# A transformer layer and a graph-attention layer in fp32: four projections by seven products of quarters, attention in 8 units instead of 12

## The chip, the cores and the metric

The kernel runs on one core of a Trainium2 chip. The metric is the device time of one launch in microseconds (us). The engines are named as in the profile: PE (TensorE), DVE (VectorE), ACT (ScalarE), POOL (GpSimd).

## The reference

There are 32 independent batches of 512 rows and 512 features, all in fp32, with a sparse adjacency matrix of 512 x 512 that is shared by all of them.

```python
# x (32, 512, 512), adj (512, 512); 8 heads of 64
h = relu(layernorm(x))
q, k, v = h @ Wq + bq, h @ Wk + bk, h @ Wv + bv          # per head below
attn = softmax(q @ k.T / 8 + (1 - adj) * -1e9)
x = x + (attn @ v) @ Wo + bo
h = relu(layernorm(x))                                    # layer 1
g = h @ W
e = leaky_relu(g @ a1 + (g @ a2).T, 0.2) * adj
h_prime = softmax(e) @ g
x = x + elu(h_prime + beta * g)
```

Per batch there are four projections (q, k, v and Wo), attention in four pairs of heads, and for layer 1 a gather (`pg`) and a last product (`py`).

## The kernel before

Batches are pipelined. While batch b does its attention, batch b+1 is projected, batch b-1 goes through Wo and its second normalisation, and batch b-2 ends. TensorE's order is written by hand. The order of the other engines is set at build time by a scheduler, from its own estimate of when each operand is ready. VectorE, ScalarE and GpSimd then take their instructions in that order: in this kernel's trace 3323, 1670 (activations and copies) and 1517 of them stand in the order of the built program, none out of it.

The names in the profiles are those of tiles: `pn` are the transposes of x ahead of the projections (the "turn" in the code), `ps` the scores, `e` the masked scores and then their exponentials, `es` the sums of these, `po` the values, `pd` the denominators, `pbs` a row of logits spread over all rows.

```python
psum = ... bufs=2                      # three tags: mm (1 bank), s (2 banks), o (1 bank), two buffers each

def product(nc, out, lhsT, rhs, start=True, stop=True):      # two halves of 64 columns side by side
    for s in range(0, out.shape[0], HD):
        nc.tensor.matmul(out[s : s + HD], lhsT[:, s : s + HD], rhs, start=start, stop=stop)

def proj_k(b, hT, f, kT):                                    # one of 4 blocks; q, v and Wo alike
    p = psum.tile([P, N], F32, name=f"pk_{b}_{f}", tag="mm")
    for c in range(C):
        product(nc, p, wk[:, c, ts(f, P)], hT[c], start=c == 0, stop=c == C - 1)
    k = wtile([P, N], f"kT_{b}_{f}", "kT", 6)
    nc.scalar.activation(k, p, AF.Identity, bias=bk_c[:, f : f + 1])

def scores(b, j, k, st):
    p = psum.tile([P, 2, N], F32, name=f"ps_{b}_{j}_{k}", tag="s")
    ...                                                       # two matmuls of 512 columns
    e = wtile([P, 2, N], f"e_{b}_{j}_{k}", "e", 6)
    nc.vector.tensor_tensor(e, p, nmT[:, k, :]..., op=ALU.add)   # adds the mask, frees the bank
    nc.scalar.activation(e, e, AF.Exp)
    ...                                                       # GpSimd sums e over k into es

# attention: 12 units a batch, three per pair of heads; dense groups are spread evenly between them
units.append(lambda j=j: (scores(b, j, 0, s), scores(b, j, 1, s)))
units.append(lambda j=j: attend(b, j - 1, s))
units.append(lambda j=j: (scores(b, j, 2, s), scores(b, j, 3, s)))

def norm0(b, xs):                                             # layer norm ahead of the projections
    for t in range(T):
        ...                                                   # DVE statistics, POOL power of -0.5
        nc.vector.tensor_scalar(xs[t], xs[t], mv[:, 0:1], rstd, op0=ALU.subtract, op1=ALU.mult)
```

After Wo, each of the four row blocks has its normalisation: statistics on DVE, a power on POOL, a relu on ACT, and two reductions `scr` on DVE. The logits of layer 1 follow (`at`, eight DVE instructions and four exponentials).

Of the kernel before, what the change touches and what calls it, by code (L numbers as in the profile page):

```python
# [17 lines left out]
P = 128  # L18
# [15 lines left out]
def product(nc, out, lhsT, rhs, start=True, stop=True):  # L34


    for s in range(0, out.shape[0], HD):
        nc.tensor.matmul(out[s : s + HD], lhsT[:, s : s + HD], rhs, start=start, stop=stop)  # L38
# [8 lines left out]
def kernel(  # L47
# [34 lines left out]
    wq, wk, wv, wo, w1 = (ctile([P, C, D], n) for n in ("wq", "wk", "wv", "wo", "w1"))  # L82

    def load_w(w, ap):
        nc.scalar.dma_start(w, ap.rearrange("(c p) f -> p c f", p=P))
# [27 lines left out]
    def row_bcast(psum, work, col, name):  # L113

        dg = work.tile([P, T, P], F32, name="dg" + name, tag="dg", bufs=1)
        nc.vector.tensor_tensor(
            dg, ident.unsqueeze(1).to_broadcast([P, T, P]),
            col.unsqueeze(2).to_broadcast([P, T, P]), op=ALU.mult,
        )
        p = psum.tile([P, N], F32, name="pb" + name, tag="mm")  # L120
        product(nc, p, ones, dg.rearrange("p t n -> p (t n)"), start=True, stop=True)
        return p
# [6 lines left out]
    psum = fast.enter_context(tc.tile_pool(name="psum", bufs=2, space=bass.MemoryType.PSUM))  # L129
# [22 lines left out]
    def masks():  # L152
        for k in range(T):
            p = psum.tile([P, N], F32, name=f"pa_{k}", tag="mm")
# [15 lines left out]
    def row_constants():  # L170

        nc.gpsimd.dma_start(c_row, bcast_rows(bo, D))
        p = psum.tile([P, D], F32, name="pc", tag="mm")
        for c in range(C):
            r = wtile([P, P], f"bvr_{c}", "y", 3)
            nc.vector.tensor_copy(r, bv_c[:, c : c + 1].to_broadcast([P, P]))
            product(nc, p, r, wo[:, c, :], start=c == 0, stop=c == C - 1)
        nc.vector.tensor_add(c_row, c_row, p)
        wa = wtile([P, 2, C], "wa", "wa", 1)
        for g in range(2):  # L180
            ar = wtile([P, D], f"a_{g}", "x1", 6)
# [36 lines left out]
    def turn(b, xs, hT, c):  # L218
        p = psum.tile([P, N], F32, name=f"pn_{b}_{c}", tag="mm")
        for t in range(T):  # L220
            nc.tensor.transpose(p[:, ts(t, P)], xs[t][:, ts(c, P)], ident)
        h = wtile([P, N], f"hT_{b}_{c}", "T", 12)
        nc.scalar.activation(h, p, AF.Relu)
        hT.append(h)

    def proj_q(b, hT, f, qT):
        p = psum.tile([P, N], F32, name=f"pq_{b}_{f}", tag="mm")
        for c in range(C):
            product(nc, p, wq[:, c, ts(f, P)], hT[c], start=c == 0, stop=c == C - 1)
        q = wtile([P, N], f"qT_{b}_{f}", "qT", 6)  # L230
        nc.vector.scalar_tensor_tensor(  # L231
            q, p, bq_c[:, f : f + 1], edge8, op0=ALU.add, op1=ALU.mult
        )
        qT.append(q)

    def proj_k(b, hT, f, kT):
        p = psum.tile([P, N], F32, name=f"pk_{b}_{f}", tag="mm")
        for c in range(C):
            product(nc, p, wk[:, c, ts(f, P)], hT[c], start=c == 0, stop=c == C - 1)
        k = wtile([P, N], f"kT_{b}_{f}", "kT", 6)  # L240
        nc.scalar.activation(k, p, AF.Identity, bias=bk_c[:, f : f + 1])  # L241
        kT.append(k)

    def proj_v(b, hT, t, v):
        p = psum.tile([P, D], F32, name=f"pv_{b}_{t}", tag="mm")
        for c in range(C):
            product(nc, p, hT[c][:, ts(t, P)], wv[:, c, :], start=c == 0, stop=c == C - 1)
        s = wtile([P, D], f"v_{b}_{t}", "v", 8)
        nc.scalar.mul(s, p, VS)
        v.append(s)  # L250

    def scores(b, j, k, st):

        p = psum.tile([P, 2, N], F32, name=f"ps_{b}_{j}_{k}", tag="s")
# [5 lines left out]
        e = wtile([P, 2, N], f"e_{b}_{j}_{k}", "e", 6)  # L260
# [5 lines left out]
        if k == 1:  # L266
            st["es"][j] = wtile([P, 2, N], f"es_{b}_{j}", "es", 2)
# [5 lines left out]
    def attend(b, j, st):  # L273

        po = psum.tile([P, N], F32, name=f"po_{b}_{j}", tag="o")
        e, v = st["e"][j], st["v"]
        for k in range(T):
            for s in range(2):
                nc.tensor.matmul(  # L279
                    po[s * HD : (s + 1) * HD, :],  # L280
                    v[k][:, (2 * j + s) * HD : (2 * j + s + 1) * HD],
                    e[k][:, s, :], start=k == 0, stop=k == T - 1,
                )
        pd = psum.tile([P, N], F32, name=f"pd_{b}_{j}", tag="o")
# [4 lines left out]
        o = wtile([P, N], f"oT_{b}_{j}", "T", 12)  # L289
        nc.scalar.copy(o, po)  # L290
        rd = wtile([P, N], f"rd_{b}_{j}", "rd", 2)
        nc.vector.reciprocal(rd, pd)  # L292
        junk = wtile([P, N], f"rj_{b}_{j}", "rj", 1)
        nc.scalar.activation(junk, rd, AF.Copy, accum_out=rsum[:, b, j : j + 1])
        nc.gpsimd.tensor_tensor(o, o, rd, op=ALU.mult)  # L295
        st["oT"].append(o)

    def residual(b, st):

        st["x1"] = []  # L300
        for t in range(T):
            r = wtile([P, D], f"x1_{b}_{t}", "x1", 6)
            nc.sync.dma_start(r, x[b, ts(t, P), :])
            nc.gpsimd.tensor_tensor(r, r, c_row, op=ALU.add)  # L304
            st["x1"].append(r)

    def out_proj(b, t, st):
        p = psum.tile([P, D], F32, name=f"pw_{b}_{t}", tag="mm")
        for c in range(C):
            product(  # L310
                nc, p, st["oT"][c][:, ts(t, P)], wo[:, c, :], start=c == 0, stop=c == C - 1
            )
        x1 = st["x1"][t]
        nc.vector.scalar_tensor_tensor(x1, p, 1.0 / VS, x1, op0=ALU.mult, op1=ALU.add)  # L314

        if t == 0:
            st["mv"] = wtile([P, T, 2], f"mv1_{b}", "mv1", 2)
        mv = st["mv"][:, t, :]
        rstd = wtile([P, 1], f"rs1_{b}_{t}", "rs1", 4)
        stats(x1, t, f"b{b}", mv, rstd)  # L320
        nb = wtile([P, 1], f"nb_{b}_{t}", "nb", 4)
        nc.vector.scalar_tensor_tensor(nb, mv[:, 0:1], -1.0, rstd, op0=ALU.mult, op1=ALU.mult)
        hn = wtile([P, D], f"hn_{b}_{t}", "hn", 4)
        nc.scalar.activation(hn, x1, AF.Relu, bias=nb, scale=rstd)  # L324
        st["hn"].append(hn)
        if t == 0:
            st["s12"] = wtile([P, 2, T], f"s12_{b}", "s12", 2)
        for g, r in ((0, wa1_r), (1, wa2_r)):
            scr = wtile([P, D], f"scr_{b}_{t}_{g}", "y", 3)
            nc.vector.tensor_tensor_reduce(  # L330
                scr, hn, r, 1.0, 0.0, op0=ALU.mult, op1=ALU.add,
                accum_out=st["s12"][:, g, t : t + 1],
            )
# [19 lines left out]
    def diagonal(b, st):  # L353

        pd = psum.tile([P, T, HD], F32, name=f"pe_{b}", tag="mm")
# [15 lines left out]
    def gather(b, c, st):  # L371
        p = psum.tile([P, N], F32, name=f"pg_{b}_{c}", tag="mm")
# [4 lines left out]
        g = wtile([P, N], f"gT_{b}_{c}", "T", 12)  # L377
# [3 lines left out]
    def final(b, t, st):  # L381
        p = psum.tile([P, D], F32, name=f"py_{b}_{t}", tag="mm")
# [10 lines left out]
        nc.gpsimd.tensor_tensor(y, y, st["x1"][t], op=ALU.add)  # L393
# [5 lines left out]
    def new_state(b):  # L399
        states[b] = {  # L400
            "x": load(b), "hT": [], "qT": [], "kT": [], "v": [], "e": [[] for _ in range(NP)], "es": {},
            "oT": [], "hn": [], "at": [], "gT": [],
        }

    def front_groups(b):
        s = states[b]
        for f in range(C):
            yield lambda f=f: proj_q(b, s["hT"], f, s["qT"])
            yield lambda f=f: proj_k(b, s["hT"], f, s["kT"])
        for t in range(T):  # L410
            yield lambda t=t: proj_v(b, s["hT"], t, s["v"])

    def dense(b):


        def of(n, make, count=4):
            if n is None:
                return [None] * count
            return [lambda i=i: make(n, i) for i in range(count)]

        nxt = b + 1 if b + 1 < B else None
        prev = b - 1 if 0 <= b - 1 < B else None
        old = b - 2 if b >= 2 else None
        s, so = states.get(prev), states.get(old)
        G = of(old, lambda n, c: gather(n, c, so))
        Y = of(old, lambda n, t: final(n, t, so))
        W = of(prev, lambda n, t: out_proj(n, t, s))
        F = list(front_groups(nxt)) if nxt is not None else [None] * 12
        V = F[8:]
        L = [(lambda: (new_state(b + 2), norm0(b + 2, states[b + 2]["x"]))) if b + 2 < B else None]  # L430
        lg = of(prev, lambda n, i: logits(n, s), 1)
        D = of(prev, lambda n, i: diagonal(n, s), 1)
        if b == B:
            order = G + Y[:2] + W + Y[2:3] + lg + Y[3:] + D + [judge]
        else:
            order = (
                G + [Y[0], F[0], Y[1], F[1], W[0], Y[2], W[1], F[2], W[2], Y[3], W[3], F[3], F[4]]
                + L + [F[5]] + lg + [F[6], F[7]] + V[:2] + D + V[2:]
            )
        return [g for g in order if g is not None]  # L440

    def attention(b):

# [268 lines left out]
```

## Time and profile before

| | before |
|---|---|
| time, median | 4039.0 us (4037.9 to 4042.4, 4 runs) |
| steady period, one batch | 123.29 us (28 periods) |
| everything else (start and end) | 586 us |
| TensorE busy | 96% |
| half clock in the steady part | 13.7 us in all |

The "period" is the distance between the transposes `pn` of successive batches in TensorE's timeline. Here it is taken over the 28 batches from the fourth on, because the steps before and after those lack one stage of the pipeline or another. These are rows of the page's costliest groups. Behind the bar stand the busy time, the mean of one in ns, and the idle time just before them with what ended most of it.

```profile
L261 DVE TENSOR_TENSOR e<-ps,nmT 128x1024 f32<-128x1024 f32 x512 | 606.7, 1216 | 431.0 <-PE ps L257 419.6
L257 PE MATMUL ps<-qT,kT 64*128 64x512 f32 x2048 | 522.4, 625 | 6.1 <-DVE e L261 4.1
```

VectorE waits 420 us for scores, while TensorE waits 4.1 us in the whole run for a bank that VectorE has to free.

### The profile page before, as it was taken

The page shows a single profiled execution, that of the slowest core. Times are in us where ns is not written, and L with a number is a line of the kernel's source. Part 1 is how long each engine was busy: PE and PEld are TensorE (multiplying, and loading weights), DVE is VectorE, ACT ScalarE, POOL GpSimd, SP SyncE. Part 2 cuts the span into 40 slices and gives each one's busy share as a digit, 9 for nine tenths or more (in the row PEclk, how much of TensorE's full clock was granted, in tenths as well). Part 3 has the DMA queues.
Part 4 walks back from the last instruction along what each step waited for, and adds up shares of the span by engine and source line. Part 5 has one row for each costly group of instructions (what it writes and reads, how often), then busy time and mean ns, then how long its engine had stood idle before and what let it go on. Part 6 is the DMA issues. An engine that isn't in the chain of part 4 may idle for free. (4 is left out here: it accounts for less than half of the span.)

```text
span 4038.4 us, 45341 instructions
## 1 busy us (share of the span) xinstructions
PE 3886.6 (96%) x18094; PEld 1303.7 (32%) x18094; DVE 2428.3 (60%) x3323; ACT 1258.4 (31%) x1799; POOL 1843.7 (46%) x1519
## 2 busy tenths in 40 slices
PE   6999999999999999999999999999999999999977
PEld 2333333333333333333333333333333333333322
DVE  4556665566655566655666555666556665556653
ACT  1333323333223333333332233333333322333331
POOL 2444544445444445444444444454444444444451
PEclk9999999999999999999999999999999999999989
DMA  3000010001010000110000100001000000000000
GB/s 117 11 17 26 22 32 27 27 21 32 22 32 27 27 22 22 32 30 23 22 32 21 32 27 26 23 21 32 32 21 22 32 21 32 27 27 11 21 21 27
DMA packets 59100, 110.75 MB, mean 27 GB/s; under 512 B 6465, under 2 KB 6465, under 8 KB 58881
## 3 DMA queue, kind: packets, MB, share of 16 engines
q1 hardware_dynamic: 55872, 101.74, 8.1%
q10 hardware_dynamic: 2640, 5.24, 0.4%
q8 instruction: 144, 2.36, 0.3%
q0 software_dynamic: 368, 0.79, 0.1%
q14 instruction: 76, 0.61, 0.1%
HBM read 74.19 MB, written 33.55 MB: 27 GB/s over the span
## 5 line engine op out<-in xcount | busy, mean ns | idle before, releaser
L271 POOL TENSOR_TENSOR es<-es,e 128x512 f32<-128x512 f32 x512 | 715.0, 1427 | 447.5 <-ACT e L264 447.5
L261 DVE TENSOR_TENSOR e<-ps,nmT 128x1024 f32<-128x1024 f32 x512 | 606.7, 1216 | 431.0 <-PE ps L257 419.6
L264 ACT ACTIVATE e<-e 128x1024 f32<-128x1024 f32 x512 | 540.6, 1056 | 906.9 <-DVE e L261 869.2
L292 DVE RECIPROCAL rd<-pd 128x512 f32<-128x512 f32 x128 | 429.4, 3355 | 430.5 <-PE pd L286 430.5
L257 PE MATMUL ps<-qT,kT 64*128 64x512 f32 x2048 | 522.4, 625 | 6.1 <-DVE e L261 4.1
L38 PE MATMUL pq<-hT,wq 128*64 128x512 f32 x2048 | 464.6, 596 | 13.9 <-ACT kT L241 12.9
L38 PE MATMUL py<-w,gT 128*64 128x512 f32 x2048 | 467.6, 599 | 0.5 <-DVE qT L231 0.5
L271 POOL TENSOR_TENSOR es<-e,e 128x512 f32<-128x512 f32 x256 | 344.7, 1368 | 267.6 <-ACT e L264 267.6
L38 PE MATMUL pw<-wo,oT 128*64 128x512 f32 x2048 | 462.8, 594 | 3.3 <-DVE x L314 3.3
L38 PE MATMUL pk<-hT,wk 128*64 128x512 f32 x2048 | 463.0, 594 | 1.1 <-DVE at L341 1.1
L279 PE MATMUL po<-e,v 128*64 128x512 f32 x2048 | 462.6, 594 | 0.0
L38 PE MATMUL pg<-at,hn 128*64 128x512 f32 x2048 | 453.7, 596 | 0.0
L38 PE MATMUL pv<-wv,hT 128*64 128x512 f32 x2048 | 450.8, 593 | 0.0
L295 POOL TENSOR_TENSOR oT<-oT,rd 128x512 f32<-128x512 f32 x128 | 172.0, 1344 | 598.3 <-DVE rd L292 530.8
L304 POOL TENSOR_TENSOR x<-x,c_row 128x512 f32<-128x512 f32 x128 | 166.1, 1299 | 393.4 <-DMA x<-in_x_dram 349.5
L330 DVE CUSTOM_DVE_ANT_0 scr<-hn,wa_r 128x512 f32<-128x512 f32 x256 | 277.7, 1121 | 64.8 <-ACT hn L324 64.6
L393 POOL TENSOR_TENSOR y<-y,x 128x512 f32<-128x512 f32 x128 | 162.4, 1269 | 290.4 <-DVE y L392 290.4
L257 PEld LDWEIGHTS ps<-qT,kT 64*128 64x128 f32 x2048 | 176.5, 188 | 328.0 <-issue 222.1
L391 DVE TENSOR_SCALAR y<-y 128x512 f32<-128x512 f32 x128 | 124.6, 974 | 242.8 <-ACT y L390 242.8
L38 PEld LDWEIGHTS pq<-hT,wq 128*64 128x64 f32 x2048 | 141.3, 137 | 321.0 <-issue 259.6
L38 PEld LDWEIGHTS pw<-wo,oT 128*64 128x64 f32 x2048 | 147.0, 137 | 298.0 <-issue 291.6
L279 PEld LDWEIGHTS po<-e,v 128*64 128x64 f32 x2048 | 147.4, 138 | 292.8 <-issue 292.2
(95 smaller groups left out, 3153.3 us busy)
## 6 DMA issues: line engine op xcount, KB each, us to landing
x<-in_x_dram SPq DMA_DIRECT2D x256, 256.0 KB, 3.0
out_dram<-y SPq DMA_DIRECT2D x128, 256.0 KB, 3.0
wq<-in_L_gnn_Wq_dram ACTq DMA_DIRECT2D x1, 1024.0 KB, 6.9
wk<-in_L_gnn_Wk_dram ACTq DMA_DIRECT2D x1, 1024.0 KB, 14.2
adj<-in_adj_dram SPq DMA_DIRECT2D x4, 256.0 KB, 11.9
wv<-in_L_gnn_Wv_dram ACTq DMA_DIRECT2D x1, 1024.0 KB, 12.2
wo<-in_L_gnn_Wo_dram ACTq DMA_DIRECT2D x1, 1024.0 KB, 14.4
w<-in_L_gnn_W_dram ACTq DMA_DIRECT2D x1, 1024.0 KB, 13.0
```

The source lines that it names most:

```text
L38: nc.tensor.matmul(out[s : s + HD], lhsT[:, s : s + HD], rhs, start=start, stop=stop)
L257: nc.tensor.matmul(p[:, s, :], st["kT"][j][rows, ts(k, P)], st["qT"][j][rows, :], start=True, stop=True)
L261: nc.vector.tensor_tensor(e, p, nmT[:, k, :].unsqueeze(1).to_broadcast([P, 2, N]), op=ALU.add)
L264: nc.scalar.activation(e, e, AF.Exp)
L271: nc.gpsimd.tensor_tensor(es[:, s, :], one[:, s, :], e[:, s, :], op=ALU.add)
L279: nc.tensor.matmul(po[s * HD : (s + 1) * HD, :], v[k][:, (2 * j + s) * HD : (2 * j + s + 1) * HD], e[k][:, s, :], start=k == 0, stop=k == ...
L292: nc.vector.reciprocal(rd, pd)
L295: nc.gpsimd.tensor_tensor(o, o, rd, op=ALU.mult)
L304: nc.gpsimd.tensor_tensor(r, r, c_row, op=ALU.add)
L330: nc.vector.tensor_tensor_reduce(scr, hn, r, 1.0, 0.0, op0=ALU.mult, op1=ALU.add, accum_out=st["s12"][:, g, t : t + 1],)
L391: nc.vector.tensor_scalar(y, y, 1.0, -1.0, op0=ALU.min, op1=ALU.add)
L393: nc.gpsimd.tensor_tensor(y, y, st["x1"][t], op=ALU.add)
```

## The change

Strassen's method (in Winograd's form) makes a product of 2 x 2 blocks with seven block products, not eight, and more additions. Here blocks are 256 x 256. The products are accumulated in PSUM, and partial results are handed on by ScalarE copies between banks ("seeds"). The blocks of the weights are combined once, those of the tokens once per batch on GpSimd. Seven blocks of each weight matrix take more SBUF than the four that make up the matrix, and the ring of exponentials shrinks from 6 to 4. The attention is recut in 8 units, each of two scores and half of the values, so that fewer exponentials live at once (this reason is read from the diff). The diff, cut to its core:

```diff
-    psum = fast.enter_context(tc.tile_pool(name="psum", bufs=2, space=bass.MemoryType.PSUM))
+    psum = fast.enter_context(tc.tile_pool(name="psum", bufs=1, space=bass.MemoryType.PSUM))
...                                                  # tags now: x, y, po, pd (1 bank each), s, qz (2 banks each)
+    def combos(b, name, pairs, tag):
+        b11, b12, b21, b22 = (block(pairs, k) for k in range(4))
+        t2, t3, t4 = (wtile([P, 2, H], f"{name}{i}_{b}", tag, 3) for i in (2, 3, 4))
+        nc.gpsimd.tensor_tensor(t3, b22, b12, op=ALU.subtract)
+        nc.gpsimd.tensor_tensor(b12, b12, b11, op=ALU.subtract)
+        nc.gpsimd.tensor_tensor(t2, b22, b12, op=ALU.subtract)
+        nc.gpsimd.tensor_tensor(t4, t2, b21, op=ALU.subtract)
...
+    def seven(name, w, B, tokens, one, two):
...                                                  # times(): 8 matmuls of 256 columns, 16 records in the profile
+        x_ = tile1("x")
+        times(x_, A11, "b11", True)
+        y_ = tile1("y")
+        nc.scalar.copy(y_, x_)
+        yield
+        qz = psum.tile([P, 2, N], F32, name=f"qz_{name}", tag="qz")
+        z_ = qz[:, 1, :]
+        times(qz[:, 0, :], S1, "t1", True)
+        q_ = wtile([P, N], f"q5_{name}", "q5", 1)
+        nc.scalar.copy(q_, qz[:, 0, :])
+        yield
+        times(y_, S2, "t2", False, onto=True)
+        nc.scalar.copy(z_, y_)
+        yield
+        times(x_, A12, "b21", False, onto=True)
+        one(0, 0, x_)
+        yield
+        times(z_, S3, "t3", False, onto=True)
+        two(1, 1, z_, q_)
+        yield
+        times(y_, S4, "b22", False, onto=True)
+        two(0, 1, y_, q_)
+        yield
+        times(z_, NA22, "t4", False, onto=True)
+        one(1, 0, z_)
...
-        e = wtile([P, 2, N], f"e_{b}_{j}_{k}", "e", 6)
+        e = wtile([P, 2, N], f"e_{b}_{j}_{k}", "e", 4)
...
+    def unit(b, n, tags=("qz", "s")):
+        s = states.get(b)
+        j, second = divmod(n, 2)
+        if s is not None:
+            for k in range(2):
+                scores(b, j, 2 * second + k, s, tags[k])
...
+    def step(b):
...
+        def strassen(pieces, n=1, between=None):
+            for i, _ in enumerate(pieces):
+                if i == 0:
+                    att(n, ("qz", "s"))              # a unit after the first product
+                if i == 4 and between:
+                    between()
...                                                  # v, unit 1, gather and final with units 2 to 4
+        if nxt is not None:
+            turn(b + 1, nxt)
...
+        if prev is not None:
+            strassen(out_proj(b - 1, prev))          # unit 5
...
+        if b + 2 < B:
+            new_state(b + 2)
+            norm0(b + 2, states[b + 2]["x"])
+        if nxt is not None:
+            strassen(proj_k(b + 1, nxt))             # unit 6
+        if prev is not None:
+            logits(b - 1, prev)
+        if nxt is not None:
+            strassen(proj_q(b + 1, nxt))             # unit 7
```

## The prediction

> **What bounds the kernel now.** I read the page's first two parts for the bound, then TensorE's waits, then the timeline for where a batch spends its time.
>
> ```profile
> PE 3886.6 (96%) x18094; PEld 1303.7 (32%) x18094; DVE 2428.3 (60%) x3323; ACT 1258.4 (31%) x1799; POOL 1843.7 (46%) x1519
> PE   6999999999999999999999999999999999999977
> PEclk9999999999999999999999999999999999999989
> L38 PE MATMUL pk<-hT,wk 128*64 128x512 f32 x2048 | 463.0, 594 | 1.1 <-DVE at L341 1.1
> ```
>
> TensorE is busy all the way, at full clock; the loads of weights (PEld) lie under it. A busy PE is not proof, so I ask what it waits for:
>
> ```profile
> PE pbs L38 <- DVE qT L231: 51.5, 28, 3.2
> PE pn L221 <- DVE x L214: 21.6, 1, 21.6
> PE pe L38 <- POOL as L351: 13.0, 2, 8.7
> PE pq L38 <- ACT kT L241: 12.9, 24, 0.5
> ```
>
> Beside the start and the end, TensorE waits only 1.8 us (51.5 / 28) and 0.5 us in a batch. So it is bound by the number of columns that it streams. The transposes pn, once a batch, start at 1985.85, 2108.95 and 2231.87 us in the timeline; over 28 batches (260.3 to 3712.5) the period is 123.3 us. Start and end take the other 586 us.
>
> The pitch, from the PE timeline:
>
> ```profile
> 2001.67 7.04 PE L38 MATMUL pg<-at,hn 128*64 128x512 f32 x32
> 2008.63 1.99 PE L257 MATMUL ps<-qT,kT 64*128 64x512 f32 x8
> 2101.47 0.69 PE L38 MATMUL pe<-ones,as 128*64 128x64 f32 x16
> 2101.99 1.46 PE L38 MATMUL pv<-wv,hT 128*64 128x512 f32 x6
> ```
>
> Each half of 64 columns is two records, and two halves run side by side. 32 records take 6.96 us from start to start, less some 0.1 us for the change of tile form: 429 ns for a side-by-side pair of 512 columns. 16 records of 64 columns take 0.52 us, 58 ns in the steady part. A line through both gives 217 ns for a pair of 256 columns (an estimate: 5 ns fixed, 0.83 ns a column).
>
> [...]So halving the columns loses almost nothing. [...]after a wait of 3.19 us (pbs at 1461.76) the clock was 0.50 for 3.41 us. [...]scr takes 626 to 1779 ns, the long ones beside POOL work.
>
> **The change part by part.**
>
> Removed: a projection was 64 records of 512 columns, 32 pairs x 429 = 13.74 us. Seven products of 16 records of 256 columns are 56 pairs x 217 = 12.17 us. Four projections a batch: 6.3 us saved, 201 us in all. TensorE's own need falls from 119.5 to 113.2 us: 48.7 for projections, 27.5 for gather and final, 33.4 for eight units of attention (scores 1.92, half of the values 1.8, denominators 0.86 every second unit), 3.6 for the small ones. The units' count moves no work; it sets how far apart scores stand.
>
> Added on other engines, per batch: three ScalarE copies of 580 ns a projection, 7.0 us; eight GpSimd combinations of 1.3 to 1.4 us, 11 us, and four half-width multiplications, 3 us; VectorE some 5 us (kT and v partly moved to it, two more adds for x1). Busy would be DVE 81, POOL 72, ACT 44 of some 125 us: none becomes the bound by its sum. The seeds (copy of x into y, of y into z) have a 1.74 us product between them and their use, against about 0.8 us for copy and semaphore: hidden, when the engine's queue is free.
>
> Moved, and this decides: scores had two buffers of two banks beside two banks for projections. Now one of their two buffers, qz, is also where Strassen's products go, and each scores unit in a projection puts its first tile into qz. The next product must wait until VectorE has added the mask to that tile. VectorE takes its instructions in the built order. I read this order for one batch: in front of the mask-add of unit 6 (in the k projection, just after Wo) stand all of the normalisation after Wo, four rows, and nearly all of that before the batch after next. Before, a row of it stood between projections.
>
> The groups that matter there:
>
> ```profile
> L330 DVE CUSTOM_DVE_ANT_0 scr<-hn,wa_r x256: 626/694/1779, 190.6 to 3986.5; 128x512 f32<-128x512 f32 x128
> L195 DVE BATCH_NORM_STATS2 st_b<-x x128: 686/695/698, 186.5 to 3983.0; 128x6 f32<-128x512 f32 x128
> 2060.90 0.68 DVE L195 BATCH_NORM_STATS2 st_a<-x 128x6 f32<-128x512 f32 x1
> 2077.31 2.34 DVE L261 TENSOR_TENSOR e<-ps,nmT 128x1024 f32<-128x1024 f32 x2
> ```
>
> I walk from the end of Wo's sixth product, where y is complete, with start-to-start times (a little under durations). VectorE: semaphore 0.2; two adds 1.3; add from z 0.65; eight statistics x 0.6 = 4.8; eight reductions scr x 0.62 = 5.0, undisturbed; twenty small ones 1.5; two of the four scalings of x 0.95; the mask-add 1.2; waits for GpSimd's power some 0.7: 16.3 us. TensorE meanwhile has the seventh product 1.74, k's first 1.74, scores 1.92, values 1.8, denominators 0.86, and 0.4 for z: 8.4 us. It then stands for **7.9 us in each batch**, before k's second product.
>
> Others found in the same walk: Wo's first product writes the bank x, which the last transposes have just filled, and ScalarE's four relus (0.6 each) end 1.25 us after them: 1.25 us. In the q projection, the mask-add of unit 7 stands behind the eight logits instructions (pbs to the last: 5.1 us, some 7 with GpSimd's sums beside them), and TensorE has only 5.5 us of work: 3.0 us. z of Wo: 0.45 us. [...]the clock will halve in most batches; some 3.4 us of work at half speed cost 1.7 us.
>
> Sum: 113.2 + 7.9 + 1.25 + 3.0 + 0.45 + 1.7 = 127.5 us a batch against 123.3. Over 28 batches +118 us. Start and end: four batches of smaller products, -25 us; masks through one bank, back-to-back units in the first step, and a longer normalisation chain in the last, +15 to +20. Prediction 4150 us.
>
> **The rivals.** First: the saving arrives. If VectorE had the mask-add done in time, only small waits would remain: 113.2 + 5 = 118 us, 3890 us in all. For it: VectorE is busy 60% and 65% after, and before the trace shows scores hardly ever waiting (ps for e 4.1 us in all). Against it: in the timeline of before, the scores that ended by 2072.1 got their mask-add at 2077.31. VectorE was already 5 us behind at this very place, and a second buffer hid it.
>
> Second: GpSimd becomes the pace. 58 us become 72, [...]eight scr at 1.7 instead of 0.65 would be +8 us, the stand near 16 us, the time 4370 us. Against it: by the walk GpSimd has ended the sums of unit 5 before the normalisation begins, and only the short powers are left. In the trace of before a power came late once a batch (3.34 us behind es), so some of it may come.
>
> Third: the stand is real but partly paid back, because VectorE's backlog is worked off and the waits before pbs (1.8 us) are gone. I have counted their absence already. Without the clock's fall it would be 4100 us, which counts as the same.
>
> **Range and chances.** 1 us a batch is 28 us. I give the period plus or minus some 4.5 us, mostly for the stand and the clock: 4010 to 4290. Faster by over 2% needs a period below 120.6, that is the stand almost gone; the durations used are already the undisturbed ones, so 0.12, for a misread order. Within 2% (120.6 to 126.4): 0.33. Slower: 0.55.
>
> **What would show it.** Right: a row of qz of the k projection waiting for e (DVE) about 30 times with 6 to 10 us each; PEclk below 9 in many slices; the seven products' rows near 390 us each for Wq, Wk, Wv, Wo instead of 460; PE's share near 90%; a smaller wait of qz of q for e; x of Wo waiting for ACT hT near 1.2 us. Wrong: pitch of pairs of 256 columns well above 217 ns (then no saving at all); waits of TensorE under 5 us a batch (first rival); scr means above 1.3 us with POOL near full beside them (second rival); ScalarE's copies (y or qz) as the main releaser.

## The result

The changed kernel is correct and took 4155.1 us (median of 4 runs, 4154.6 to 4157.9) against 4039.0 us. The ratio is 1.0287, with a 95% interval of 1.027 to 1.0305: slower. A ratio is the mean time of one kernel's fast runs over the mean of the other's fast runs of the same rounds, so it is not quite the ratio of the medians quoted. The prediction said 4150 us and slower with 0.55.

The busy line and two slices of the page of the changed kernel:

```profile
PE 3737.9 (90%) x24302; PEld 1771.4 (43%) x24302; DVE 2362.5 (57%) x3712; ACT 1402.5 (34%) x2119; POOL 2180.0 (52%) x1922
PE   5998999988999888999889999889998889998977
PEclk7999999999999999999999999999999999999998
```

TensorE's busy time fell by 149 us while the span grew by 118 us. TensorE was given less to do and does it later. No engine is near full, so the time must lie in waits. TensorE's waits in the changed kernel (engine, waiting tile, releaser: total us, times, longest):

```profile
PE qz_k L46 <- DVE e L400: 212.5, 30, 7.5
PE qz_q L46 <- DVE e L400: 47.6, 30, 1.6
PE pn L275 <- ACT hT L283: 25.9, 32, 1.6
...
PE x_w L46 <- ACT hT L286: 21.4, 29, 0.7
PE qz_k L46 <- POOL hT L263: 12.3, 1, 12.3
```

The first row is the one foreseen: k's second product waits until VectorE has added the mask to a tile of scores. Of its 30 times 28 lie in the steady part and take 7.5 us each (210.3 / 28); the 7.1 us that the expectations below name is the mean with two short ones of the start and end. Its place in TensorE's timeline (start, duration, and in brackets the idle time before it with its releaser):

```profile
2127.21 1.90 PE L46 MATMUL qz_w<-wo,uT 128*64 128x256 f32 x16
2128.94 1.90 PE L46 MATMUL x_k<-hT,wk 128*64 128x256 f32 x16
2130.88 1.99 PE L396 MATMUL ps<-qT,kT 64*128 64x512 f32 x8
...
2134.56 1.03 PE L431 MATMUL pd<-es,ones 128*64 128x512 f32 x4
2143.10 3.68 PE L46 MATMUL qz_k<-hT,wk 128*64 128x256 f32 x16 [7.51 <-DVE e L400]
2146.57 2.13 PE L46 MATMUL y_k<-tT,wk 128*64 128x256 f32 x16
```

A product has a pitch of 1.73 us (2127.21 to 2128.94), 216 ns for each of its eight pairs. So the saving in TensorE's work is real. The scores were complete by about 2132.8. After the stand of 7.51 us the next product takes 3.68 us instead of 1.90: the granted clock is 0.50 from 2140.2 to 2147.0 us. The two products from 2143.10 to the third at 2148.53 take 5.43 us where two pitches are 3.46, which makes 1.97 us lost. VectorE's timeline of the same stretch shows what stood in front of the mask:

```profile
2128.88 1.29 DVE L227 BATCH_NORM_STATS2 st_b<-x 128x6 f32<-128x512 f32 x2
...
2132.67 0.66 DVE L493 CUSTOM_DVE_ANT_0 scr<-hn,wa_r 128x512 f32<-128x512 f32 x1
...
2139.24 0.66 DVE L227 BATCH_NORM_STATS2 st_a<-x 128x6 f32<-128x512 f32 x1
...
2140.62 1.16 DVE L246 TENSOR_SCALAR x<-x,mv,rs 128x512 f32<-128x512 f32 x2
...
2141.85 1.19 DVE L400 TENSOR_TENSOR e<-ps,nmT 128x1024 f32<-128x1024 f32 x1
```

This is one queue: the reductions `scr` after Wo, among and behind them the statistics `st_a` and the scaling of `x` for the batch after next, and only then the mask. The trace shows the order kept: the scores lay ready from about 2132.8 us, and the mask-add waited its turn for 9 us. Over the steady part:

| us per batch | before | after, predicted | after, measured |
|---|---|---|---|
| TensorE's own work | 119.5 (estimate); 120.7 (what its waits of 1.8 and 0.5 us and the clock leave) | 113.2 | 113.6 (what the other rows leave) |
| k's second product for the mask-add | - | 7.9 | 7.5 |
| q's second product for the mask-add | - | 3.0 | 1.6 |
| transposes, and Wo's first product, for the relu | - | 1.25 | 0.8 + 0.7 |
| Wo's z | - | 0.45 | not in the list |
| lost to the half clock | 0.2 (half of 13.7 / 28) | 1.7 | 2.0 |
| period | 123.3 | 127.5 | 126.3 |
| start and end together, us | 586 | 576 to 581 | 620 |

### The profile page after: what moved, and what is told of

It is laid out like the page before. It is cut to its first block, busy times and chain, and to the rows that moved or that the text cites. A ratio compares the mean times of both kernels' runs of the same rounds, so it can differ in the third digit from the quotient of the medians.

```text
span 4156.0 us, 59252 instructions
## 1 busy us (share of the span) xinstructions
PE 3737.9 (90%) x24302; PEld 1771.4 (43%) x24302; DVE 2362.5 (57%) x3712; ACT 1402.5 (34%) x2119; POOL 2180.0 (52%) x1922
## 4 chain that ended last, share of the span: by engine, by line
PE 69%; DVE 20%; POOL 5%; issue 3%; ACT 2%; DMA 1%; DVEq 0%; POOLq 0%; ACTq 0%
PE pg L46 10%; PE ps L396 8%; PE po L419 8%; PE py L46 5%; PE qz_k L46 5%; PE qz_q L46 4%; PE qz_v L46 4%; DVE scr L493 3%; PE x_v L46 3%; PE y_k L46 3%; PE y_v L46 3%; PE y_q L46 3%; DVE x L464 3%; DVE rd L439 3%; PE x_w L46 3%
## 5 line engine op out<-in xcount | busy, mean ns | idle before, releaser
L410 POOL TENSOR_TENSOR es<-es,e 128x512 f32<-128x512 f32 x512 | 638.0, 1278 | 319.0 <-ACT e L403 319.0
L419 PE MATMUL po<-e,v 128*64 128x512 f32 x2048 | 497.2, 606 | 2.9 <-ACT e L403 2.4
L230 POOL TENSOR_TENSOR rs<-rs,mhalf 128x1 f32<-128x1 f32 x256 | 157.0, 619 | 378.1 <-DVE rs L229 264.0
L46 PE MATMUL qz_k<-hT,wk 128*64 128x256 f32 x512 | 112.4, 616 | 224.8 <-DVE e L400 212.5
L46 PEld LDWEIGHTS pg<-at,hn 128*64 128x64 f32 x2048 | 148.8, 138 | 299.4 <-issue 295.9
L46 PEld LDWEIGHTS py<-w,gT 128*64 128x64 f32 x2048 | 147.8, 137 | 291.7 <-issue 291.7
L556 DVE TENSOR_SCALAR y<-y 128x512 f32<-128x512 f32 x128 | 83.7, 654 | 309.1 <-ACT y L555 309.1
L512 POOL TENSOR_TENSOR as<-at,at 128x512 f32<-128x512 f32 x32 | 40.7, 1271 | 306.7 <-ACT at L508 306.7
L46 PEld LDWEIGHTS qz_k<-hT,wk 128*64 128x64 f32 x512 | 53.0, 216 | 286.6 <-DVE e L400 238.9
L555 ACT ACTIVATE y<-py,rd 128x512 f32<-128x512 f32 x128 | 87.5, 683 | 246.8 <-PE py L46 182.6
```

Of the source, the lines that this page charges most:

```text
L230: nc.gpsimd.tensor_tensor(rstd, rstd, mhalf[:, 0:1], op=ALU.pow)
L410: nc.gpsimd.tensor_tensor(es[:, s, :], one[:, s, :], e[:, s, :], op=ALU.add)
L419: nc.tensor.matmul(po[s * HD : (s + 1) * HD, :], v[k // 2][:, k % 2, (2 * j + s) * HD : (2 * j + s + 1) * HD], e[k][:, s, :], start=k == 0 ...
```

## The experiments

Twelve kernels were run, all with three rounds against the kernel before on the same chip; all gave correct results. "Half" is the time at half clock within the 28 steady periods.

| run | median us | ratio to before (95%) | period | half, us |
|---|---|---|---|---|
| the change | 4155.1 | 1.0287 (1.0270 to 1.0305) | 126.27 | 191 |
| a_norm0_late | 3987.6 | 0.9861 (0.9844 to 0.9877) | 120.11 | 0 |
| f_units | 4117.0 | 1.0185 (1.0168 to 1.0202) | 124.47 | 140 |
| h_all | 4051.6 | 1.0020 (1.0004 to 1.0037) | 122.43 | 96 |
| d_pool_more | 4180.1 | 1.0336 (1.0318 to 1.0353) | 126.88 | 208 |
| k_start | 4146.0 | 1.0263 (1.0246 to 1.0280) | 126.27 | 191 |
| n_a_plus | 3946.8 | 0.9767 (0.9751 to 0.9784) | 118.80 | 0 |
| m_best | 3976.4 | 0.9836 (0.9819 to 0.9852) | 119.82 | 17 |
| e_units_alone | 4199.8 | 1.0390 (1.0373 to 1.0407) | 128.76 | 160 |
| r_before_buffers | 4026.9 | 0.9967 (0.9950 to 0.9983) | 122.49 | 0 |
| p_split | 4033.2 | 0.9980 (0.9964 to 0.9997) | 122.19 | 79 |
| q_split_both | 4080.9 | 1.0096 (1.0079 to 1.0113) | 123.88 | 137 |
| s_pscale | 4018.9 | 0.9939 (0.9917 to 0.9960) | 122.04 | 120 |

### a_norm0_late: the normalisation moved out of VectorE's queue

The theory was the stand in VectorE's queue. The rivals were that it would only move, and that GpSimd set the pace. The edit moves one call and changes no arithmetic:

```diff
         if b + 2 < B:
             new_state(b + 2)
-            norm0(b + 2, states[b + 2]["x"])
...                                                  # next step, after its second unit
         att()
+        if b >= 1 and nxt is not None:
+            norm0(b + 1, nxt["x"])
```

> The normalisation of the batch after next is called one step later in the program; the scheduler then builds VectorE's order so that in front of the mask-add of unit 6 stand no longer its eight instructions of that norm (some 4.0 us) and four of the eight reductions scr (2.45 us). Theory (the mask-add queues behind VectorE's normalisation, and TensorE cannot reuse bank pair qz): the wait of qz of the k projection for e falls from 7.1 to about 1 us a batch, the half-clock windows vanish, a new wait of up to 2.3 us appears at k's seventh product for kT (now behind the reductions and the reciprocal). Period 126.3 to about 120.3 us, time about 3985 us (3940 to 4040). Rival (GpSimd's extra work or Strassen's seeds set the pace): GpSimd and ScalarE do the same work, so within 1% of 4155 us.

It took 3987.6 us, 4% less than the change and 1.4% less than the kernel before. TensorE's waits:

```profile
PE qz_q L46 <- DVE e L400: 56.3, 30, 1.9
PE qz_k L46 <- DVE kT L371: 51.7, 30, 2.7
PE qz_k L46 <- DVE e L400: 27.1, 30, 1.2
```

The first wait of the changed kernel fell from 7.5 to 0.9 us a batch, and a wait of 1.7 us came up behind it: k's seventh product, for k's additions on VectorE. The half clock vanished from the steady part. With waits of 7.5 us each batch had 6.83 us (191 / 28) at half clock, and here, where no steady wait is above 1.9 us, none. Shorter ones than 7.5 us came with half clock too: four of the five waits of 2.25 to 3.19 us in the steady part of the kernel before were followed by it (see the last section), and q_split_both, with waits of 3.0 us (85.6 / 29), had 137 us of it. The period fell by 6.16 us. TensorE's listed waits in the steady part account for 10.7 - 6.1 = 4.5 of it (before rounding), which leaves 1.6 for the clock, where the timeline above gave 1.97; the 0.3 between them was not traced.

One reservation: VectorE's built order moved more than the edit names. In this run the first mask-add stands ahead of the last four reductions `scr` as well, because the scheduler sorts by its estimate of readiness. So the run shows that the queue ahead of the mask-add is the cause. It does not share it out between the two normalisations.

### f_units and h_all: the units moved away from k, then away from q

In f_units, a unit is issued before the transposes and none in k. In h_all, in addition, the normalisation is late as above, unit 7 stands ahead of the logits, and two relus of the turn are merged.

```diff
# f_units
+            att()                                   # one more unit before the turn
-            strassen(proj_k(b + 1, nxt))
+            strassen(proj_k(b + 1, nxt), n=1 if old is None else 0)
# h_all, besides a_norm0_late and f_units
+        if old is not None:
+            att()                                   # unit 7 ahead of the logits
         if prev is not None:
             logits(b - 1, prev)
-            strassen(proj_q(b + 1, nxt))
+            strassen(proj_q(b + 1, nxt), n=1 if old is None else 0)
```

> Nothing but the place of attention's units: unit 5 before the turn, unit 6 inside Wo's products, none inside the k projection; VectorE's normalisation stays as it was and where it was. Theory: the wait of k's second product for e (7.1 us a batch) is gone, but k's seventh product must wait for kT, which now stands behind the same normalisation: about 3.7 us. Two thirds of the stand go at most: period 120.5 to 122.5, time about 4020 us (3980 to 4070). Rival (the units' place does not matter, GpSimd or the engines' sums do): within 1% of 4155 us.

> Both of these, unit 7 moved from the q projection to before the logits, and the relu of the first two transposes as one instruction. Theory: of the waits of 7.1, 1.6, 0.8 and 0.7 us a batch about 1.7 (kT) and 0.7 remain, no half clock: period about 117 us, time 3885 us (3840 to 3960), 4% faster than the kernel before: the 201 us saved by the seven products at last arrive. Rival (Strassen costs elsewhere what it saves): not under 4000 us.

Both theories missed, at 4117.0 and 4051.6 us. These times lie where the rivals put them (within 1% of 4155; not under 4000), but f_units not for its rival's reason, for the wait that was aimed at did go. One row of the waits of each, f_units first:

```profile
PE qz_k L46 <- DVE kT L371: 107.7, 29, 3.8
```

```profile
PE qz_q L46 <- ACT qz_q L319: 102.5, 29, 3.6
```

In f_units k's products no longer wait for the mask-add (one wait of 0.7 us in the whole run). But the normalisation is still in VectorE's queue and now meets k's additions, and the transposes wait 1.8 us a batch (56.7 / 32) for relus that stand behind unit 5's exponentials on ScalarE. In h_all the waits of k are nearly gone (10.9 us in all), and q's seed, a ScalarE copy, now stands behind the exponentials of the logits. The wait that I took away was replaced by the next instruction in a queue, and the new waits, at 3.8 and 3.6 us each, halved the clock in most batches (140 and 96 us over the 28).

### d_pool_more: more work for GpSimd

This tests the second rival of the prediction, that GpSimd sets the pace. One combination is done three times, on the projections' tokens and on Wo's alike.

```diff
-        nc.gpsimd.tensor_tensor(t3, b22, b12, op=ALU.subtract)
+        for _ in range(3):
+            nc.gpsimd.tensor_tensor(t3, b22, b12, op=ALU.subtract)
```

> The changed kernel with GpSimd's first combination of each set done three times over (same values): four more GpSimd instructions of 1.28 us a batch, 5 us, 164 us in all, right results. Theory (GpSimd is not on the path): time within 0.5% of 4155 us. Rival (GpSimd is the pace or blocks VectorE where it matters): longer by 2 to 5 us a batch, 4215 to 4300 us.

GpSimd's busy time rose by 190 us (128 more instructions; 164 us had been expected) and the kernel took 25 us longer (0.6%, a little outside the expectation). The first wait stayed at 212.0 us. GpSimd is not the pace; its work is not quite free: the scores' wait that the profile puts down to VectorE's `rs` rose from 1.7 to 20.1 us, and the half clock from 191 to 208 us.

### k_start: the start

The combinations of three weight matrices move from GpSimd to VectorE.

```diff
-        combine(nc.gpsimd, wq, aq)
+        combine(nc.vector, wq, aq)
...                                                  # wv and wo alike
```

> The changed kernel, with the combinations of weight quarters moved from GpSimd to VectorE and nothing else altered. Theory (the start lost time because some 22 us of weight combinations stand on GpSimd ahead of the first batch's token combinations, so that k's second product waits 12.3 us): that wait goes, the first batch begins earlier, the steady period stays at 126.3 us and the time falls by 12 to 25 us, to about 4137. Rival (the start is bound by something else, the loads or the half clock, and the wait only moves): within 5 us of the changed kernel, 4150 to 4160.

It took 4146.0 us, 9 us less than the change, at the same period. The single wait of 12.3 us for GpSimd is gone. So small a difference lies within the intervals of the two ratios; the runs themselves do not overlap (4144.0 to 4151.9 against 4154.6 to 4157.9), and in the profiled runs start and end took 608 us for 620. The expectation was 12 to 25, so this cause is real and smaller than I thought: by the medians it is about a quarter of the 34 us by which start and end grew. Of the rest, the profiles show what it is made of, not why. At half clock the start has 55 us in place of 14 and the end 50 in place of 40, which costs up to 25 us (half of the difference). TensorE's idle time there is 38 us more. Against these stand the 25 us that the smaller products of four batches save. What would shorten the start further stays open.

### n_a_plus and m_best: the best version

n_a_plus is a_norm0_late with the weight combinations on VectorE, the merged relu, and the third step's transposes in another bank. m_best adds the move of units of f_units.

```diff
# n_a_plus, besides a_norm0_late and k_start
-            nc.scalar.activation(h[0][:, c, :], p[:, c, :], AF.Relu)
+        nc.scalar.activation(h[0], p, AF.Relu)      # once, after both
-        p = psum.tile([P, N], F32, name=f"pn3_{b}", tag="x")
+        p = psum.tile([P, N], F32, name=f"pn3_{b}", tag="pd")
```

> The changed kernel with the normalisation of the batch after next behind the attention's unit 7 on VectorE (as in the run that gave 3988), plus three small repairs: the weight combinations on VectorE, the third step's transposes into a bank that does not wait for the relu, and the relu ahead in ScalarE's queue where the order allows. Theory (waits of single PSUM banks and the order of the queues are what held the saving back): the waits at the turn (26.1 and 21.4 us in all) mostly go, period about 118.6 us, time about 3930. Rival (the waits at the turn only hid one another, and what is left is the queue of ScalarE): period 119.5 to 120.1, time 3965 to 3990.

> As the run before it in this set, and with the last half of unit 5 moved so that k's products no longer meet the addition of the mask. Theory: the waits of k's products (0.9 and 1.7 us per batch) go too, half-clock windows become rarer, period 116.7 to 118 us, time 3890 to 3930. Rival (unit 5's exponentials now stand ahead of the relu on ScalarE, as they did when the units alone were moved): pn waits 1.5 to 2 us per batch, period 119 to 120, time no better than the run before it.

n_a_plus took 3946.8 us at a period of 118.80 us where about 3930 and 118.6 were expected. It beats the kernel before by 2.3% and the change by 5%. Its steady waits:

```profile
PE qz_q L46 <- DVE e L400: 56.2, 30, 1.9
PE qz_k L46 <- DVE kT L371: 54.5, 31, 2.9
PE qz_k L46 <- DVE e L400: 27.3, 30, 1.2
```

The waits for the relus, 26.1 and 21.4 us before, have left the list. With one more of 0.6 us (scores for a step of the normalisation), the waits sum to 5.2 us. The period less these is 113.6 us, with no half clock, so TensorE's own need was predicted (113.2 us) to within 0.4%. This is the cleanest measurement of what the seven products give: against 120.7 us in the kernel before, TensorE needs 7.1 us less a batch (6.3 were predicted), and the period keeps 4.5 of it.

m_best was meant to be better and took 3976.4 us. Two rows of its waits:

```profile
PE qz_q L46 <- DVE e L400: 72.2, 30, 2.5
PE pd L431 <- POOL es L410: 36.5, 41, 3.5
```

k's waits did fall (14.3 us in all), and q's grew. With units back to back, the denominators now wait for GpSimd's sums. The rival's numbers came (a period of 119 to 120, no better than the run before), but its cause, exponentials ahead of the relu, is only part of it (16.7 us for Wo's first product). The list does not explain the loss either: in the steady part TensorE stands idle 4.6 us a batch here and 5.2 in n_a_plus, and the period is 1.0 us longer. The timeline shows where the list is blind:

```profile
2025.51 1.86 PE L431 MATMUL pd<-es,ones 128*64 128x512 f32 x3 [0.83 <-POOL es L410]
2026.74 0.65 PE L46 MATMUL qz_w<-wo,oT 128*64 128x256 f32 x2
2027.21 0.59 PE L431 MATMUL pd<-es,ones 128*64 128x512 f32 x1
```

One record of the denominators comes after the next product has begun, and as I read it Wo's products then run with their two halves of 64 columns out of step: while one half waits and the other works, TensorE does not count as idle. By subtraction (119.8 - 4.6 of idle time - 0.3 of clock - 113.6) some 1.3 us a batch go there, an estimate that no run tested.

### e_units_alone and r_before_buffers: the units without the products

The kernel before with its attention in the 8 units and all products as they were. With the original rings this would deadlock (by my own account; no run shows it), and two were altered (12 to 14, which the expectation misstates as 16 to 14, and 6 to 5). The second run is the control, with 12 units and the altered rings.

```diff
-            units.append(lambda j=j: (scores(b, j, 0, s), scores(b, j, 1, s)))
...                                                  # three units per pair of heads
+        def unit(n):                                # two per pair: two scores, half of the values
+            j, second = divmod(n, 2)
+            for k in range(2):
+                scores(b, j, 2 * second + k, s)
+            ...
```

> The kernel before, all products as they were, with its attention in 8 units and not 12 (two rings of buffers cut, 16 to 14 and 6 to 5, so that it fits). Theory (the cut into units moves no work and matters only because it decides where VectorE's additions of the mask fall against the products): the work of TensorE is the same, time within 1% of the kernel before, 4000 to 4080. Rival (the units themselves cost the time that the products save): 4100 or more.

> Control for the run of the 8 units alone: the kernel before in its 12 units, with only the two rings of buffers altered (12 to 14 and 6 to 5). Theory (the loss of 159 us in that run comes of the cut into units, by the order on VectorE, and not of the rings): within 1% of the kernel before, 4000 to 4080. Rival (one ring less of exponentials holds the attention up): 4100 or more, with waits of TensorE or ScalarE that name the ring.

My theory fell and the rival held: 4199.8 us, and the rings are not to blame, for the control took 4026.9, even 0.3% less than the kernel before. The units alone cost 6.3 us a batch (128.76 - 122.49). Two rows of the waits of e_units_alone:

```profile
PE pbs L38 <- DVE qT L231: 113.1, 28, 5.1
PE pk L38 <- DVE y L396: 37.7, 29, 2.3
```

They are again waits for VectorE, 4.0 and 1.3 us a batch, and 160 us at half clock where the control has none. All waits of TensorE (5.6 us a batch for 1.9 in the control) and the clock (up to 2.9) make up the loss. "The units' count moves no work" was true, and as a statement about time it was wrong. Why the waits grow was not tested; my reading is that dense groups fall into 8 gaps and not 12, and VectorE's pieces with them in larger lumps. So in the change as a whole, the cut into units is not a neutral part. How much of the change's own stand is due to it cannot be read off by subtraction, since that kernel's order was made anew.

### p_split, q_split_both and s_pscale: three attempts beyond the best

p_split takes the second half of the logits out of the queue ahead of unit 7's mask. q_split_both moves half of the normalisation after Wo behind unit 6's mask as well. s_pscale is p_split with four scalings on GpSimd.

```diff
# p_split
-            logits(b - 1, prev)
+            logits(b - 1, prev, (0, 1))
-            strassen(proj_q(b + 1, nxt))
+            strassen(proj_q(b + 1, nxt), late=... logits(b - 1, prev, (2, 3)))    # after q's sixth product
# q_split_both, besides
-            if i == 1:
-                norm1(b, st, (0, 1))
+            strassen(proj_k(b + 1, nxt), ..., first=... norm1(b - 1, prev, (0, 1)))   # after unit 6
# s_pscale, besides p_split
-            nc.vector.tensor_scalar(
+            nc.gpsimd.tensor_scalar(
                 xs[t], xs[t], mv[:, 0:1], rstd, op0=ALU.subtract, op1=ALU.mult
```

> As the run that gave 3947, with the logits cut in two halves, of which the second is issued inside q's products. Theory (unit 7's masked scores stand behind eight operations of the logits on VectorE, and q's second product waits for them, 1.9 us a batch; two of the eight now come after): that wait falls to about 0.6 us, period about 117.5 us, time about 3910. Rival (what is taken off there comes back as a wait for q's additions or ScalarE's copies behind the later exponentials): no change, 3935 to 3960.

> As the run before it in this set, with the normalisation of the first two row blocks after Wo behind unit 6's additions of the mask on VectorE. Theory: the wait of k's second product for them (0.9 us a batch) goes and the wait for k's additions (1.8 us) stays, period about 116.5 us, time 3880 to 3900. Rival (the normalisation now stands ahead of k's additions and the wait for those grows by as much): 3910 to 3950.

> As the run with the logits in two halves (4033), with the four scalings of x before the turn on GpSimd instead of VectorE. Theory (in that run VectorE waited 6.3 us in its order for GpSimd's power, which stood behind four sums of exponentials, and q's additions behind it): VectorE no longer meets that wait, the wait of q's products for its additions goes from 3.6 us a batch to under 1, period about 117.5 to 118.5 us, time 3905 to 3945. Rival (GpSimd's queue itself is late by then, and q's multiplications there hold the next scores): period above 120 us, 3990 or more, with scores or denominators waiting for GpSimd.

All three lost to n_a_plus: 4033.2, 4080.9 and 4018.9 us. p_split shows why. The aimed-at wait is gone from its list, and this row leads, in the place that its rival named but larger than that allowed:

```profile
PE qz_q L46 <- DVE qT L351: 101.8, 28, 3.6
```

VectorE's timeline and GpSimd's at that place (one batch; idle time and releaser in brackets):

```profile
2096.16 1.99 DVE L246 TENSOR_SCALAR x<-x,mv,rs 128x512 f32<-128x512 f32 x2 [6.26 <-POOL rs L230]
2099.64 0.86 DVE L351 SCALAR_TENSOR_TENSOR qT<-y_q,bq_c,q_q 128x256 f32<-128x256 f32 x2
```

```profile
2088.46 5.93 POOL L410 TENSOR_TENSOR es<-es,e 128x512 f32<-128x512 f32 x4 [1.68 <-ACT e L403]
2094.34 1.28 POOL L516 TENSOR_TENSOR as<-as,at 128x512 f32<-128x512 f32 x1
2095.57 1.17 POOL L230 TENSOR_TENSOR rs<-rs,mhalf 128x1 f32<-128x1 f32 x2
```

A power on 128 single numbers stands behind four sums of exponentials on GpSimd. VectorE waits 6.26 us for it before it may scale x, q's additions stand behind that scaling, and TensorE waits 3.6 us for those: two queues in series. s_pscale tested this reading by taking the scaling off VectorE. The wait for q's additions left the list as expected, and the rival's came in its place:

```profile
PE ps L396 <- POOL qT L354: 94.0, 28, 3.4
```

GpSimd itself is late there, and its multiplications for q hold the scores. In q_split_both the seed of k (85.6 us for ACT's copy) and q's additions (87.4 us) took over. p_split and s_pscale removed the wait that they were aimed at; q_split_both hardly did (k's second product still waits 0.8 us for the mask-add, 23.8 / 30, after 0.9). Each uncovered the next queue, and each new wait was some 3 us or more (3.6, 3.0 and 3.1, 3.4); with them the half clock came back (79, 137 and 120 us).

## Why the prediction was right, and where it was not

**What bounds the kernel, and the saving.** Right. The pitch of a pair of 256 columns was 216 ns against 217, and TensorE's need 113.6 us, in the change and in n_a_plus, against 113.2. The need of the kernel before was put too low, 119.5 us for 120.7, so the saving was 7.1 us and not 6.3.

**The stand before k's second product.** Right in place, cause, count and size: 7.5 us for 7.9. a_norm0_late shows the cause, VectorE's queue. The difference is in the walk: from the end of Wo's sixth product (2127.4) to the release (2143.1) VectorE took 15.7 us for 16.3, and TensorE's work in it 8.2 for 8.4.

**The other waits.** q's was mis-sized, 1.6 us for 3.0. The relu's was 0.7 us at Wo for 1.25, and 0.8 us more at the transposes themselves, which I had not listed. Wo's z (0.45) never appeared.

**The half clock.** Right: 2.0 us for 1.7, and a_norm0_late shows that it goes with the stand. That it would halve in most batches was an estimate, from one wait of 3.19 us and the 3.41 us at 0.50 after it; it did in all 28, for 6.83 us each. In the batch shown TensorE worked at half speed for 3.9 us (2143.1 to 2147.0), where some 3.4 had been put. One sign did not come: PEclk stays at 9 in all slices but the first and the last, as 6.83 us in 126.3 leave the mean of a steady batch at 0.97.

**Start and end.** This step failed. "Start and end: four batches of smaller products, -25 us; masks through one bank, back-to-back units in the first step, and a longer normalisation chain in the last, +15 to +20." Measured: +34 us, where the sum gives -5 to -10. A quarter is the weight combinations ahead of the first tokens on GpSimd (k_start). The greater part is a slower clock and more idle time, whose cause stays open. The total of 4150 came so near 4155 because two misses cancel: the period was 1.2 us shorter than predicted (-34 us over 28 batches), the ends some 42 us longer. That is luck, and "slower" is part of it: the prediction counts a period of 120.6 to 126.4 us as within 2%, and 126.27 lies there. With the ends as predicted the time would have been 28 x 126.27 + 578.5 = 4114 us, 1.9% over the kernel before.

**The rivals.** The first, that the saving arrives, did not come true for this kernel, and its estimate (3890 us at a period of 118 us) is nearly what n_a_plus does in the steady part (118.8). The second, GpSimd, was wrong twice: the mean of `scr` fell from 1121 to 686 ns, as GpSimd's sums no longer fall beside it in the timeline (180 of 256 `scr` ran beside a GpSimd instruction on a tile of 512 columns before, 3 of 256 in the change), and more work on GpSimd hardly mattered. The third was counted in already.

**Two small slips of its sums.** Eight units of attention come to 33.2 us, not 33.4 (8 x 3.72 + 4 x 0.86), and the range of 4010 to 4290 is plus or minus 5 us a batch, not 4.5. Neither moves the result.

**What the prediction lacked.** It treated the cut into 8 units as neutral. e_units_alone shows 6.3 us a batch in the kernel before for that alone.

## What to carry to other kernels

When one engine is busy 96% of the time, less work for it pays only if the engines that free its banks are on time, so read the built order of their queues at the place where a bank has lost its second buffer. A late engine need not be a busy one: VectorE was 57% busy here, and one instruction stood 9 us behind work that was not urgent. Remove the longest wait first, above all one over some 2 us, since in the steady part of the kernel before four of five waits of 2.25 to 3.19 us were followed by half clock and none of 2.0 us or less, and in the change all 28 stands of 7.5 us came with it; and measure after each step, because six other attempts here (f_units, h_all, m_best, p_split, q_split_both, s_pscale) mainly uncovered the next queue.

## What the traces show of the hardware

- The clock. In the steady part of the kernel before, waits of TensorE of 2.25, 3.19, 2.98 and 2.96 us (they begin at 473.21, 1458.58, 2321.72 and 3185.53 us) were each followed by 3.41 us at a granted clock of 0.50, 13.7 us in all. After one of 2.57 us (2569.93) the clock stayed at 1.00, as it did after all of 2.0 us or less. A stand that recurs at 7.5 us cost 6.83 us at half clock and 2.0 us of lost work each time.
- The pitch of fp32 matmuls in halves of 64 columns side by side: a pair took 216 ns at 256 columns and 429 ns at 512. In the kernel before, 16 records of `pw` took 3.43 us from start to start when the next product had the same form and 3.53 us when scores followed (medians of 39 each), which is the 0.1 us that the prediction takes off for a change of form.
- The 0.2 us that the prediction takes for a semaphore: in the kernel before, an idle VectorE or ScalarE that waited for a product began 0.22 us after TensorE had begun its next work (median 217 ns in 192 and 316 cases).
- The order of a queue, in an engine that is not full: an instruction ready at 2132.8 us ran at 2141.85, with its engine 57% busy over the run. All 3712 instructions of VectorE in this trace stand in the order of the built program.
- GpSimd's time for a small instruction: a power on 128 x 1 numbers took 554 ns (n_a_plus, median of 256), and in p_split it stood behind 5.93 us of sums.
- VectorE beside GpSimd: in the kernel before, `scr` took 1304 ns on average in the 180 cases that ran beside a GpSimd instruction on a tile of 512 columns, and 689 ns in the 76 that did not.
